# z and v on lanes of patch half and pixel in a convolution-and-GRU kernel: VectorE turns their product, GpSimd applies the norm's weight and bias

## The chip, the cores and the metric

The kernel runs as one program on one core of a Trainium2 chip. Five engines work side by side, each through its own queue in order: TensorE (PE, with its weight loads listed apart as PEld), VectorE (DVE), ScalarE (ACT), GpSimd (POOL) and SyncE (SP), which issues DMAs. The metric is the device time of one execution in microseconds (us). The time before is 5713.79 us, the median of three runs (5709.91 to 5723.35).

## The reference

The input x is (4, 64, 256, 256) in float32. Two residual layers follow each other.

```python
# layer 0
g = groupnorm(x)                                  # 32 groups, no weight
hidden = depthwise3x3(w1 @ g)                     # 64 -> 384 channels
q, k, v = split(hidden, 3)                        # 128 channels each
out = irfft2(rfft2(patches8x8(q)) * rfft2(patches8x8(k)))   # circular convolution in 8x8 patches
out = (out - mean_c(out)) / sqrt(var_c(out) + 1e-5) * ln_w + ln_b    # over the 128 channels of a pixel
x = x + w_out @ (v * out)
# layer 1
x = x + gru_over_columns(groupnorm(x))            # a scan over 256 columns, three neighbours each
```

The part in question is the norm over 128 channels, the gate `v * out`, and the projection by w_out with the residual. The normalised and gated values must get from one layout to another: the circular convolution leaves pixels on the partitions (lanes), and the projection contracts over channels, which therefore have to be on the lanes.

## The kernel before

Layer 0 runs in 32 blocks (`NBLK`) of 32 image rows, 128 patches of 8x8 pixels each. Layer 1 follows and is not touched. Every instruction is issued through a wrapper (`InOrder`, line 146) which keeps each engine's instructions in the order in which the program writes them, so the order of the Python statements is the order in each queue. All instructions carry line 158 in the profile; they are told apart by the names of their tiles.

A block n goes through these stages, in this order.

- Pointwise chunk 0, 1 and 2 (`pointwise`, line 353): 16 units each. A unit multiplies four patch columns by w1 into two PSUM banks, and ACT or VectorE copies them to h. The flag `vector` says which of the two copies.
- Circular stage 0, after chunk 0, and circular stage 1, after chunk 1 (`circular`, line 413). Each has four steps `sp`. A step transforms 16 channels of q and of k (two `transform`, 64 matmul records each) and VectorE multiplies them: three instructions `pr`, which the prediction calls a product set. ACT copies q from PSUM first; k stays in PSUM, except in the last step. Two steps together make an `inverse` (line 430), which goes back to pixels and is copied by ACT into z. It is issued one or more steps later (`pending`, `flush`).
- Values, after chunk 2 (`values`, line 450): eight steps k make v in the same layout as z. Beside them the next block's input xq is normalised (`normalize`, line 314: three quarters on ACT, one on VectorE; GpSimd sets the borders to zero).
- The norm over channels (`layer_norm`, line 469) is a generator. Each `next(norm)` in the main loop issues one more piece of it: VectorE's statistics of z during circular stage 1 and chunk 2; the mean and the variance, each through a matmul with the constant hh and back, during values; then 16 VectorE instructions on z (subtract the mean, multiply by the reciprocal root), from values into chunk 0 of the next block.
- Finish (`finish`, line 622), after chunk 0 of the next block: for each of four units u, PE transposes z and v, 128x128 at a time (`gate`, line 524). ACT applies ln_w and ln_b while it copies the transposed z, VectorE multiplies by the transposed v from PSUM, PE projects with w_out (`project`, line 566), VectorE adds to the residual xr loaded from x and takes statistics for layer 1, and SP stores to x1.

Before the change, z and v have pixels and half of the channels on the lanes: lane = channel half t x 64 pixels, columns = 128 patches x 64 channels. One lane therefore sees half of a pixel's channels, and hh joins the two halves.

PSUM is one ring of eight banks (`psum`, line 301). A pointwise unit or a transform takes two of them, an inverse four. PE can run ahead of the copies only as far as the ring is free. Work tiles come from a pool of seven. The matrices t of the transforms are loaded by SP four ahead of their use (`fetch`, line 340).

For images after the first, statistics of the next image are taken beside layer 0: GpSimd's queue loads pieces of x (`look`), and VectorE counts them (`count`).

Of the kernel before, what the change touches and what calls it, by code (L numbers as in the profile page):

```python
# [36 lines left out]
def channel_z(t, f):  # L37


    pair, rest = divmod(f, 16)  # L40
    c, s = divmod(rest, 4)
    return (2 * pair + t) * 16 + 4 * s + c
# [121 lines left out]
def tile_conv_then_gru(  # L164
# [10 lines left out]
    hh: bass.AP,  # L175
# [37 lines left out]
    with tc.tile_pool(name="xa", bufs=5) as xa, tc.tile_pool(name="sta", bufs=1) as sta, tc.tile_pool(  # L213
# [51 lines left out]
        ident = const.tile([P, P], F32, tag="ident", name="ident")  # L265
        make_identity(tc.nc, ident)
        hh_sb = const.tile([P, P], F32, tag="hh", name="hh_sb")
        nc.sync.dma_start(hh_sb, hh)
# [4 lines left out]
        wo_sb = const.tile([P, 2, C], F32, tag="wo", name="wo_sb")  # L273
        nc.sync.dma_start(wo_sb, w_out.rearrange("a f t c -> (a f) t c"))
        ln_sb = const.tile([P, 2, 2], F32, tag="ln", name="ln_sb")
        nc.sync.dma_start(ln_sb, ln.rearrange("a f n t -> (a f) n t"))
# [16 lines left out]
    with layer0 as s:  # L293
# [17 lines left out]
        z = big.tile([P, NP, NS], F32, tag="z", name="z")  # L311
        v = big.tile([P, NP, NS], F32, tag="v", name="v")
        lnst = big.tile([P, 2, NP // 2, 6], F32, tag="lnst", name="lnst")
# [63 lines left out]
        pending, later = [], []  # L377
# [35 lines left out]
        def circular(n, a, beside):  # L413
            ready = []
            for sp in range(4):
                ready.append(products(n, a, sp))
                beside(sp)
                if sp in (0, 2):
                    flush()
                if sp % 2:  # L420
                    at, pair = (n, 2 * a + sp // 2), ready[-2:]
                    pending.append(lambda at=at, pair=pair: inverse(*at, pair))
                    while later:
                        later.pop(0)()
# [5 lines left out]
        def inverse(n, pair, prods):  # L430

            pz = psum(4)
            for i in range(2):
                for part in range(2):
                    for t in range(2):
                        for c in range(4):
                            at = slice(32 * c, 32 * c + 32)
                            nc.tensor.matmul(
                                pz[t * 64 : t * 64 + 64, c, :],
                                lhsT=g_sb[at, part, i, :],  # L440
                                rhs=prods[t][i][at, part, :],
                                start=i == part == 0,
                                stop=i == part == 1,
                                tile_position=(32 * c, t * 64),
                            )
            nc.scalar.copy(
                z[:, :, 16 * pair : 16 * pair + 16], pz.rearrange("p x (f n) -> p n (x f)", n=NP)
            )

        def values(n, k, pv):  # L450

            m = matrix(n, 2, k)
            for f in range(8):
                for t in range(2):
                    nc.tensor.matmul(
                        pv[t * 64 : t * 64 + 64, f // 4, (f % 4) * P : (f % 4) * P + P],
                        lhsT=m[0:HALO, 2 * f + t, :],
                        rhs=h[:, 16 * k + 2 * f + t, :],
                        start=True,
                        stop=True,  # L460
                        tile_position=(0, t * 64),
                    )

        def keep_values(k, count, pv):
            nc.scalar.copy(
                v[:, :, 8 * k : 8 * (k + count)], pv.rearrange("p x (f n) -> p n (x f)", n=NP)
            )

        def layer_norm(n):

            st = lnst

            def statistics(a, p0, p1):

                for p in range(p0, p1):
                    nc.vector.bn_stats(
                        st[:, a, p, :],
                        z[:, 2 * p : 2 * p + 2, 32 * a : 32 * a + 32].rearrange("p n f -> p f n"),
                    )

            for i in range(4):
                statistics(0, 16 * i, 16 * i + 16)
                yield
            statistics(1, 0, 8)
            yield
            statistics(1, 8, 50)
            yield
            statistics(1, 50, NP // 2)
            m = work(f"lnm_{n}", (P, 8, NP))
            total, mean, d, var, rstd = m[:, 0], m[:, 1], m[:, 2:4], m[:, 4], m[:, 5]  # L490
            by = st.rearrange("p a i (e k) -> p a (i e) k", e=2)
            nc.vector.tensor_tensor(total, by[:, 0, :, 1], by[:, 1, :, 1], ALU.add)
            yield
            pm = psum()
            nc.tensor.matmul(pm[:, 0, 0:NP], lhsT=hh_sb, rhs=total, start=True, stop=True)
            nc.vector.tensor_copy(mean, pm[:, 0, 0:NP])
            nc.vector.tensor_tensor(
                d,
                by[:, :, :, 1],
                mean.rearrange("p (x n) -> p x n", x=1).to_broadcast([P, 2, NP]),  # L500
                ALU.subtract,
            )
            nc.vector.tensor_tensor(d, d, d, ALU.mult)
            nc.vector.scalar_tensor_tensor(d, by[:, :, :, 2], 1.0 / 32, d, ALU.mult, ALU.add)
            nc.vector.tensor_tensor(var, d[:, 0], d[:, 1], ALU.add)
            yield
            pv = psum()
            nc.tensor.matmul(pv[:, 0, 0:NP], lhsT=hh_sb, rhs=var, start=True, stop=True)
            nc.scalar.activation(rstd, pv[:, 0, 0:NP], AF.Sqrt, bias=eps, scale=1.0)
            nc.vector.reciprocal(rstd, rstd)  # L510
            yield
            for u in range(4):
                for g in range(2):
                    at = slice(g * NJ + 16 * u, g * NJ + 16 * u + 16)
                    for part, what in ((mean, ALU.subtract), (rstd, ALU.mult)):
                        nc.vector.tensor_tensor(
                            z[:, at, :],
                            z[:, at, :],
                            part[:, at].rearrange("p (n x) -> p n x", x=1).to_broadcast([P, 16, NS]),
                            what,  # L520
                        )
                    yield

        def gate(n, u):

            ys = []
            for g in range(2):
                p0 = g * NJ + 16 * u
                pz, pv = psum(), psum()
                for src, ps in ((z, pz), (v, pv)):  # L530
                    for i in range(8):
                        nc.tensor.transpose(
                            ps[:, i // 4, (i % 4) * P : (i % 4) * P + P],
                            src[:, p0 + 2 * i : p0 + 2 * i + 2, :].rearrange("p n f -> p (n f)"),
                            ident,
                        )
                y = work(f"y{g}_{n}_{u}", (P, 8, 2, 64))
                for t in range(2):
                    nc.scalar.activation(
                        y[:, :, t, :],  # L540
                        pz.rearrange("p x (i t k) -> p (x i) t k", t=2, k=64)[:, :, t, :],
                        AF.Identity,
                        bias=ln_sb[:, 1, t : t + 1],
                        scale=ln_sb[:, 0, t : t + 1],
                    )
                nc.vector.tensor_tensor(
                    y.rearrange("p i t k -> p (i t k)"),
                    pv.rearrange("p x k -> p (x k)"),
                    y.rearrange("p i t k -> p (i t k)"),
                    ALU.mult,  # L550
                )
                ys.append(y)
            return ys
# [3 lines left out]
        def residual(n, u):  # L557
            xr = work(f"xr_{n}_{u}", (P, 8, P))
            b, r0, c0 = n // 8, (n % 8) * 32 + (u // 2) * 8, (u % 2) * P
            for g in range(2):  # L560
                nc.sync.dma_start(
                    xr[g * C : (g + 1) * C], x[b, :, r0 + 16 * g : r0 + 16 * g + 8, c0 : c0 + P]
                )
            return xr

        def project(n, u, ys, xr):
            po = psum()
            for t in range(2):
                for p in range(2):
                    at = slice(p * 64, p * 64 + 64)  # L570
                    for g in range(2):
                        nc.tensor.matmul(
                            po[g * 64 : g * 64 + 64, p, :],
                            lhsT=wo_sb[at, t, :],
                            rhs=ys[g][at, :, t, :],
                            start=t == 0,
                            stop=t == 1,
                            tile_position=(p * 64, g * 64),
                        )
            grid = xr.rearrange("p r (i q c) -> p q i r c", q=2, c=8)  # L580
            for p in range(2):
                nc.vector.tensor_tensor(
                    grid[:, p],
                    po[:, p, :].rearrange("p (i r c) -> p i r c", r=8, c=8),
                    grid[:, p],
                    ALU.add,
                )
            if u == 0:
# [369 lines left out]
```

## Time and profile before

One execution was profiled.

| | us |
|---|---|
| median of three runs | 5713.79 |
| span of the profiled execution | 5733.1 |
| PE busy | 5456.4 |
| VectorE busy | 4085.7 |
| ACT busy | 3473.5 |
| GpSimd busy | 689.1 |
| layer 0's blocks, from about 130 to 4290 us: VectorE busy | 2955.9 |

The span is the time from the first to the last instruction; the page gives no other time of the profiled execution, and it stands 0.34% above the median. "Busy" counts the time in which an engine has at least one instruction under way. Matmuls are pipelined, so a busy PE is not PE at its peak. The names are read as output<-inputs: `z<-z,lnm` is a VectorE instruction that reads z and the norm's mean or factor and writes z; `psring<-h,t` is a transform or a set of values; `psring<-pr,g_sb` an inverse; `psring<-ident,z` a transpose; `psring<-y,wo_sb` a projection. A matmul in float32 leaves two records, a transpose one. In timeline rows the first two numbers are start and length in us, then engine, operation, names, shapes, count, and in brackets the idle time before and what ended it.

### The profile page before, as it was taken

The page shows a single profiled execution, that of the slowest core. Times are in us where ns is not written, and L with a number is a line of the kernel's source. Part 1 is how long each engine was busy: PE and PEld are TensorE (multiplying, and loading weights), DVE is VectorE, ACT ScalarE, POOL GpSimd, SP SyncE. Part 2 cuts the span into 40 slices and gives each one's busy share as a digit, 9 for nine tenths or more (in the row PEclk, how much of TensorE's full clock was granted, in tenths as well). Part 3 has the DMA queues.
Part 4 walks back from the last instruction along what each step waited for, and adds up shares of the span by engine and source line. Part 5 has one row for each costly group of instructions (what it writes and reads, how often), then busy time and mean ns, then how long its engine had stood idle before and what let it go on. Part 6 is the DMA issues. An engine that isn't in the chain of part 4 may idle for free.

```text
span 5733.1 us, 278945 instructions
## 1 busy us (share of the span) xinstructions
PE 5456.4 (95%) x127204; PEld 4746.7 (83%) x127204; DVE 4085.7 (71%) x9593; ACT 3473.5 (61%) x4604; POOL 689.1 (12%) x1261
## 2 busy tenths in 40 slices
PE   4999999999999999999999999999989999999999
PEld 3888888888788788888878888888869999999998
DVE  4777777777767777777776676667667777777777
ACT  3656666665566566666556656666546666666665
POOL 0000000000000000000000000000003333333333
PEclk9999999999999999999999999999999999999999
DMA  7555555555555555555555444555443333333332
GB/s 254 149 150 152 153 159 151 145 139 159 154 152 148 151 150 158 153 153 139 156 157 151 131 140 135 149 137 131 130 112 112 100 98 96 102 100 98 102 99 70
DMA packets 536798, 784.74 MB, mean 137 GB/s; under 512 B 33388, under 2 KB 427536, under 8 KB 533232
## 3 DMA queue, kind: packets, MB, share of 16 engines
q1 hardware_dynamic: 501776, 600.89, 38.6%
q0 software_dynamic: 33552, 165.43, 9.1%
q8 instruction: 996, 16.32, 1.2%
q14 instruction: 186, 1.52, 0.1%
q10 hardware_dynamic: 288, 0.58, 0.0%
HBM read 622.72 MB, written 144.05 MB: 134 GB/s over the span
## 4 chain that ended last, share of the span: by engine, by line
PE 85%; issue 4%; ACT 4%; DMA 3%; DVE 2%; POOL 0%; SPq 0%; POOLq 0%; ACTq 0%; DVEq 0%
PE psring L158 62%; PE pshz L158 8%; PE pshr L158 8%; PE psni L158 6%; DMA t<-t_all 3%; PE pshn L158 2%; ACT v L158 2%; ACT z L158 1%; ACT h L158 1%; DVE lnst L158 0%; DVE pr L158 0%; DVE z L158 0%; ACT xq L158 0%; POOL raw L158 0%; DVE n L158 0%
## 5 line engine op out<-in xcount | busy, mean ns | idle before, releaser
L158 PEld LDWEIGHTS psring<-h,t 100*32 100x32 f32 x40960 | 1334.3, 115 | 287.8 <-issue 198.4
L158 PE MATMUL psring<-h,t 100*32 100x128 f32 x40960 | 1444.2, 274 | 101.0 <-issue 36.9
L158 PEld LDWEIGHTS psring<-w_sb,xq 64*100 64x100 f32 x24576 | 1356.8, 163 | 86.8 <-issue 57.8
L158 PE MATMUL psring<-w_sb,xq 64*100 64x128 f32 x24576 | 1402.0, 271 | 25.9 <-issue 12.0
L158 ACT COPY h<-psring 100x1024 f32<-100x1024 f32 x1274 | 1206.2, 1026 | 167.9 <-PE psring L158 161.6
L158 DVE TENSOR_TENSOR pr<-psring,q 128x512 f32<-128x512 f32 (+1 forms) x576 | 462.3, 858 | 333.5 <-PE psring L158 270.5
L158 DVE BATCH_NORM_STATS2 lnst<-z 128x6 f32<-128x64 f32 x4096 | 546.0, 217 | 117.7 <-ACT z L158 117.7
L158 DVE TENSOR_TENSOR z<-z,lnm 128x1024 f32<-128x1024 f32 x512 | 612.7, 1218 | 8.8
L158 ACT COPY q<-psring 128x1024 f32<-128x1024 f32 x256 | 259.3, 1013 | 527.3 <-PE psring L158 434.3
L158 PE MATMUL pshr<-st,wi 64*64 64x144 f32 (+7 forms) x12240 | 527.7, 271 | 22.4 <-DVE st L158 13.8
L158 ACT COPY z<-psring 128x2048 f32<-128x2048 f32 x128 | 238.9, 1867 | 505.4 <-PE psring L158 505.4
L158 PE MATMUL pshz<-st,wi 64*64 64x144 f32 (+7 forms) x12240 | 527.4, 270 | 6.0 <-issue 4.7
L158 PE MATMUL psni<-st,wi 64*64 64x144 f32 (+7 forms) x12240 | 527.0, 271 | 4.4 <-issue 3.1
L158 ACT ACTIVATE z<-pshz,b_rz 128x288 f32<-128x288 f32 (+7 forms) x510 | 242.5, 476 | 462.0 <-PE pshz L158 462.0
L158 ACT ACTIVATE y<-psring,ln_sb 128x512 f32<-128x512 f32 x512 | 372.1, 780 | 201.9 <-PE psring L158 199.9
L158 PE MATMUL psring<-pr,g_sb 32*64 32x512 f32 x8192 | 486.6, 600 | 5.4 <-issue 5.4
L158 PEld LDWEIGHTS psni<-st,wi 64*64 64x64 f32 x12240 | 456.8, 133 | 30.1 <-issue 12.1
L158 PEld LDWEIGHTS pshr<-st,wi 64*64 64x64 f32 x12240 | 438.4, 133 | 37.2 <-issue 18.2
L158 PEld LDWEIGHTS pshz<-st,wi 64*64 64x64 f32 x12240 | 445.0, 133 | 15.7 <-issue 14.2
L158 DVE COPY h<-psring 100x1024 f32<-100x1024 f32 x262 | 320.1, 1222 | 171.7 <-PE psring L158 167.7
L158 DVE TENSOR_TENSOR y<-psring,y 128x1024 f32<-128x1024 f32 x256 | 312.4, 1221 | 135.3 <-ACT y L158 134.3
L158 DVE SCALAR_TENSOR_TENSOR g<-z,xn 128x288 f32<-128x288 f32 (+7 forms) x510 | 227.2, 446 | 236.3 <-ACT z L158 232.5
(101 smaller groups left out, 7536.5 us busy)
## 6 DMA issues: line engine op xcount, KB each, us to landing
t<-t_all SPq DMA_DIRECT2D x768, 400.0 KB
xq<-in_xh POOLq DMA_DIRECT2D x128, 800.0 KB, 4.6
xr<-in_x SPq DMA_DIRECT2D x256, 256.0 KB
x<-xr SPq DMA_DIRECT2D x256, 256.0 KB
raw<-x SPq DMA_DIRECT2D x128, 256.0 KB
raw<-x SPq DMA_DIRECT2D x256, 128.0 KB
out<-raw SPq DMA_DIRECT2D x128, 256.0 KB
out<-raw SPq DMA_DIRECT2D x256, 128.0 KB
```

The costliest lines, as they stand in the source:

```text
L158: return self.tc.keep_in_program_order(got(*args, **kwargs))
```

## The change

z and v now have the patch half (64 patches each) and the pixel on the lanes, and all 128 channels of 64 patches in the columns. A lane sees all the channels of its pixel. For that, the inverse and the values write 64 patches to each half of the lanes, with twice as many matmuls of half as many columns. The statistics need no matmul with hh. After VectorE has subtracted the mean and multiplied by the factor, GpSimd multiplies by ln_w and adds ln_b, both broadcast along the patches. VectorE multiplies by v in this layout and then turns the product in 32x32 blocks, in place, which puts 32 channels of a pixel group on 32 lanes. The projection contracts over 32 lanes at a time, four row groups and four channel blocks, so that two projections of 64 matmul records replace four of 16, and the 128x128 transposes on PE go.

The order changes with it. The norm's generator has 30 pieces: s0 to s7 scale one eighth of z each (two VectorE instructions, two of GpSimd), y0 to y7 multiply by v, two behind, and eight turn the product. Pieces s0 to s4 with y0 and y1 lie beside values, the other s and y beside chunk 0 of the next block (y7 after it), the turns beside circular stage 0 and the start of chunk 1. The projections move from between chunk 0 and circular stage 0 into chunk 1 (after units 0 and 7), with the loads of xr and the stores to x1. VectorE gets 12 of the 48 copies to h instead of 8.

```diff
 def inverse(n, pair, prods):
     pz = psum(4)
-    for i in range(2):
-        for part in range(2):
-            for t in range(2):
-                for c in range(4):
...
+    for t in range(2):
+        for i in range(2):
+            for part in range(2):
+                for g in range(2):
+                    for c in range(4):
+                        at = slice(32 * c, 32 * c + 32)
+                        nc.tensor.matmul(
+                            pz[g * 64 : g * 64 + 64, c, t * 256 : t * 256 + 256].rearrange(
+                                "p (s n) -> p s n", n=NJ
+                            ),
+                            lhsT=g_sb[at, part, i, :],
+                            rhs=prods[t][i][at, part].rearrange("p (s g n) -> p g s n", g=2, n=NJ)[:, g],
...
 def values(n, k, pv):
     m = matrix(n, 2, k)
-    for f in range(8):
-        for t in range(2):
+    for f in range(16):
+        for g in range(2):
             nc.tensor.matmul(
+                pv[g * 64 : g * 64 + 64, f // 8, (f % 8) * NJ : (f % 8) * NJ + NJ],
+                lhsT=m[0:HALO, f, :],
+                rhs=h[:, 16 * k + f, g * NJ : g * NJ + NJ],
...
 def layer_norm(n):
...
-    pm = psum()
-    nc.tensor.matmul(pm[:, 0, 0:NP], lhsT=hh_sb, rhs=total, start=True, stop=True)
...
+    def scaled(i):
+        at, f = where(i)
+        for part, what in ((mean, ALU.subtract), (rstd, ALU.mult)):
+            nc.vector.tensor_tensor(
+                z[:, at, f], z[:, at, f],
+                part[:, at].rearrange("p (n x) -> p n x", x=1).to_broadcast([P, 32, 32]), what)
+        for j, what in ((0, ALU.mult), (1, ALU.add)):
+            nc.gpsimd.tensor_tensor(
+                z[:, at, f], z[:, at, f],
+                ln_sb[:, j, f].rearrange("p (x f) -> p x f", x=1).to_broadcast([P, 32, 32]), what)
+
+    def gated(i):
+        at, f = where(i)
+        nc.vector.tensor_tensor(v[:, at, f], v[:, at, f], z[:, at, f], ALU.mult)
+
+    for step in "s0 s1 s2 y0 s3 y1 s4 y2 s5 y3 s6 y4 s7 y5 y6 y7".split():
+        (scaled if step[0] == "s" else gated)(int(step[1]))
+        yield
+    for i in range(8):
+        chunk = v[:, 8 * i : 8 * i + 8].rearrange("p n f -> p (n f)")
+        nc.vector.transpose(chunk, chunk)
+        yield

-def gate(n, u):
...
 def project(n, u):
+    po = psum(4)
+    y = v.rearrange("p n (b k) -> p b n k", k=32)
+    for b in range(4):
+        for r in range(4):
+            for s in range(2):
+                n0 = 32 * u + 16 * s
+                nc.tensor.matmul(
+                    po[s * 64 : s * 64 + 64, r].rearrange("p (n k) -> p n k", k=32),
+                    lhsT=wo_sb[32 * r : 32 * r + 32, b, :],
+                    rhs=y[32 * r : 32 * r + 32, b, n0 : n0 + 16],
...
 for n in range(NBLK + 1):
...
     for unit in range(16):
-        pointwise(n, 0, unit, unit in (5, 9) if norm else unit % 2)
+        pointwise(n, 0, unit, unit in (3, 8, 13) if norm else unit % 2)
+        if unit % 2:
+            go()
...
     def beside_first(sp):
+        go((2, 1, 1, 1)[sp])
...
+    go()
     circular(n, 0, beside_first)
+    if n:
+        parts[0] = residual(n - 1, 0)
...
     for unit in range(16):
-        pointwise(n, 1, unit, unit in (5, 8, 11, 14))
+        pointwise(n, 1, unit, unit in (2, 5, 8, 11, 14))
+        if unit == 0 and n:
+            po = project(n - 1, 0)
+            add_residual(0, po, parts[0])
+        if unit in (1, 3, 4, 5):
+            go()
+        if unit == 3:
+            flush()
+            if n:
+                leave(n - 1, 0, parts[0])
+                parts[1] = residual(n - 1, 1)
+        if unit == 7 and n:
+            po = project(n - 1, 1)
+            add_residual(1, po, parts[1])
+        if unit == 9 and n:
+            leave(n - 1, 1, parts[1])
...
     for unit in range(16):
-        pointwise(n, 2, unit, unit in (6, 14))
+        pointwise(n, 2, unit, unit in (1, 4, 6, 15))
...
     for k in range(8):
...
+        if k >= 1:
+            go()
```

Here `go()` issues the next piece of the norm, `add_residual` is VectorE's addition of a projection to xr, and `leave` its statistics and the stores.

## The prediction

> **What bounds the kernel now.** I read the page's busy shares, its chain, and then one block (32 alike; VectorE's reciprocals follow each other every 130.2 us on average) by windows and timeline.
>
> ```profile
> PE 5456.4 (95%) x127204; PEld 4746.7 (83%) x127204; DVE 4085.7 (71%) x9593; ACT 3473.5 (61%) x4604; POOL 689.1 (12%) x1261
> PE 85%; issue 4%; ACT 4%; DMA 3%; DVE 2%; POOL 0%; SPq 0%; POOLq 0%; ACTq 0%; DVEq 0%
> ```
>
> TensorE is busy 95% and holds 85% of the chain. In two stretches of the block at 1951 us (columns: stretch, length, then busy us of PE, weight loads, DVE, ACT, POOL, clock, DMA):
>
> ```profile
> 2036.80:2057.80 21.00, 20.74 (x371) 19.97 (x367) 20.76 (x19) 18.68 (x18) 1.35 (x6) 1.00 0.72 164
> 2057.80:2077.90 20.10, 20.10 (x182) 15.51 (x184) 16.27 (x18) 12.87 (x18) 0.00 (x0) 1.00 0.39 81
> ```
>
> The second is transposing, gating and projecting: PE full. But in the first, where z is normalised, VectorE is full too (20.76 of 21): there the two engines are even, and what is added to VectorE shows. Work by work:
>
> ```profile
> 2057.79 1.09 PE L158 MATMUL psring<-ident,z 128*128 128x128 f32 x8
> ...
> 2064.93 1.95 PE L158 MATMUL psring<-y,wo_sb 64*64 64x512 f32 x16
> 2066.80 1.09 PE L158 MATMUL psring<-ident,z 128*128 128x128 f32 x8
> ...
> 2000.27 3.69 PE L158 MATMUL psring<-pr,g_sb 32*64 32x512 f32 x64
> ...
> 2028.90 0.49 PE L158 MATMUL psring<-lnm,hh_sb 128*128 128x128 f32 x2
> 2029.32 3.71 PE L158 MATMUL psring<-h,t 100*64 100x128 f32 x64
> ...
> 2033.67 0.20 PEld L158 LDWEIGHTS psring<-h,t 100*64 100x64 f32 x4
> ...
> 2036.89 4.82 DVE L158 TENSOR_TENSOR z<-z,lnm 128x1024 f32<-128x1024 f32 x4
> ```
>
> GpSimd does no arithmetic in layer 0. How it gets on beside VectorE is seen in layer 1:
>
> ```profile
> 4905.54 0.39 POOL L158 COPY xt<-xn 64x256 f32<-64x256 f32 x1
> 4905.57 0.66 DVE L158 SCALAR_TENSOR_TENSOR g<-z,xn 128x268 f32<-128x268 f32 x1 [0.38 <-ACT z L158]
> ...
> 5086.36 0.44 DVE L158 SCALAR_TENSOR_TENSOR g<-z,xn 128x266 f32<-128x266 f32 x1 [0.51 <-ACT z L158]
> 5086.36 0.68 POOL L158 COPY xt<-xn 64x256 f32<-64x256 f32 x1
> 5086.76 0.58 DVE L158 TENSOR_TENSOR n<-n,z 128x266 f32<-128x266 f32 x1
> ```
>
> g takes 0.44 alone, 0.66 behind a copy begun 0.03 us earlier: it ends 0.30 us after the copy, which is the time of its 268 elements. At 5086 g is first, and the copy of 0.39 takes 0.68, ending 0.25 after g; n, queued next, takes 0.58 and ends 0.30 after the copy. So a VectorE instruction with two inputs in SBUF and a GpSimd instruction that reads SBUF run one after the other; only their start (0.14 us) overlaps. All 24 VectorE instructions that normalise and gate here are of that kind, and all 16 of GpSimd's.
>
> **The change part by part, per block.**
>
> *PE, removed.* 128 transposes: 64 from 2057.79 to 2064.93 and 32 in each 3.65 us after, 14.4 us. Two hh matmuls, each 0.42 to the next start: 0.8.
>
> *PE, added.* The inverse has 64 matmuls of 256 columns for 32 of 512, the same columns on eight tiles: 64 records pace at 57.6 ns now, 128 would need 28.8; the four-tile transforms come to 30 (384 records in 11.5 us): 0, at worst +0.6. The projection takes two runs of 64 records like the inverse's (7.3 us) for four of 1.87 (7.5): 0. Values: 64 columns instead of 128 and twice the records. The row of four weight loads in 0.20 us (about 0.13 each) shows the two tiles' loads side by side, a pair per 55 ns, against the 57.6 ns that a pair then needs: 0, at worst twice the stage, +14.8. I take +0.4, by that row. PE: -14.8.
>
> *ACT* loses 16 activations of 0.78 us and four h copies of 1.03. It is off the chain (4%): 0.
>
> *VectorE* trades eight multiplies y<-psring,y (1.22) for eight from SBUF (1.22), keeps 16 on z, gains four h copies (4.9) and eight block transposes. No row shows a transpose: 0.71 us by the 1600-element xq scaling (1.11), 2.05 by the 64-element statistics (128 ns apart), I take 1.22 as the tensor_tensor of the same 1024. Statistics fall from 128 by 128 ns to 64 by about 195: -3.9. Projection add and bn_stats stay eight each. The norm's small steps shrink by about 1. Busy in all: 92 us a block now (2955.9 from 130 to 4290 us, over 32), about 102 after, before any waiting.
>
> *GpSimd* gets 16 tensor_tensor of 1024. Layer 1's of 512 take 1.09 to 1.29, so 2.03 (start counted once) to 2.57. I take 2.04, as the new operands are aligned alike; 1.90 of it excludes VectorE (1.09 less 0.14, doubled).
>
> *The new wait.* Product i of v and z waits for GpSimd's two passes over block i. Behind it in VectorE's queue stand the h copies of units 3, 8 and 13, then the first product of the circular stage; PE waits for the copies' banks, for h, and for the products. Behind GpSimd's passes stand the border memsets of the next block (needed at units 4, 8 and 12) and a load of seen, which has the circular stage to land in.
>
> Count from VectorE's first instruction on z (T; 2036.89 here). If the two exclude each other: 24 of 1.09 plus 16 of 1.90 make 56.6, with the first start and the hand-overs 58, the copies and xq lying beside GpSimd. Taken in turns, the copies of units 3, 8 and 13 end near T+32, T+45 and T+52 and the last gate at T+58; the memsets are through by T+20, before they count. Then come the three instructions of the first product set (2.42), two transposes (2.4) and the second set (2.4): T+65.2, when the first inverse can start. PE now ends the pointwise at T+20.9; T comes 1.0 earlier (the variance no longer passes PE, and ACT's root is free after its first scaling of xq), so 21.9, and with six transforms (1.85 each, 11.1) PE would be there at T+33. Lateness 32.2 us. Later, in the second pointwise run, the copies behind adds and statistics hold banks: 0 to 4, I take 2.
>
> *Moved:* the projection with its eight x loads and eight x1 stores on SP goes behind the first circular stage; same count and size. Matrices are fetched four ahead of it, so 0; without that cover, waits like the 14.5 us in all that PE has on t now.
>
> Sum per block: -14.8 + 32.2 + 2 = +19.4; 31 blocks: +601. The last block has nothing beside it: from T to layer 1's norm 45.6 us now (4244.4 to 4290.0); after, 57 + 9.8 (transposes) + 14.6 (two projections at half clock) + 5.7 (adds, statistics) = 87: +41. In all +642 on the span of 5733.1: 6375; the span stands 0.34% above the median of the runs, so 6355.
>
> **The clock, weighed.** After a wait PE is slow:
>
> ```profile
> 4264.81 1.97 PE L158 MATMUL psring<-ident,v 128*128 128x128 f32 x8 [6.07 <-DVE y L158]
> ```
>
> Eight transposes take 1.97 instead of 1.04 us, the next eight 1.92. My sum pays this only in the tail: in the blocks the first four transforms end by T+61.3 even so, before the second product set needs them (T+62.8). The Trainium skill (TensorE: Matmul & The Clock Gate, "HAM oscillation") warns of gaps over about 3 us; charging 1.7 us for each of a block's three new waits would add some 158 us, an estimate by that page.
>
> **The place of the passes, weighed.** On VectorE the same 16 passes would be 16 x 1.20 = 19.3 us, and the last gate would end at T+53 instead of T+58: the rows say that GpSimd's help costs more than it saves here. The Trainium skill (GPSIMD Engine Reference, "Engine selection") sends elementwise work on a tile to VectorE and speaks against this part of the change; its 4497 ns for 2048 elements would make an estimated 2.25 us of a pass instead of 2.04, some 3 us a block more.
>
> **Rivals.**
>
> 1. *GpSimd does not hold VectorE up* (a gain). Then GpSimd's passes alone set the pace: 2.4 + 8 x 4.2 + 1.2 = 37.2, lateness 11.4, 1 for banks; -2.4 a block, -75, tail +20: about 5660. For it: the busy time that GpSimd adds, 33 us a block, is a quarter of the block. Against: the three rows above. It decides when the last gate ends by T+39.
>
> 2. *PE alone counts*, the rest hidden: -14.8 x 31 = -459, 5255. Against: VectorE's work alone from T (24 at 1.20, three copies, xq: 33.7 us) outlasts PE's 21.9, which leaves 8 us of lateness if nothing else is slow.
>
> 3. *Dearer passes*: GpSimd at 2.57 (+6.3) and a transpose at 2.05 (+1.7, and 2 for banks): +10 a block, +325 with the tail: 6680.
>
> **How the numbers follow.** Forecast 0.70; rival 1 and what lies near it 0.13, of which 0.03 falls within 0.2% (about what a measurement of this kernel can tell from no change); rival 2 0.02; rival 3 0.15. Faster 0.12, same 0.03, slower 0.85. The range goes up to rival 3, and down to a partial exclusion (the last gate at T+45: 13 us less a block, 400 in all): 5950 to 6690.
>
> **What would show it.** In the changed profile: block period near 150 us; VectorE's z and v instructions at 2 to 3 us instead of 1.22, GpSimd's at 2 to 3; PE idle on DVE h and DVE pr after each block's values, over 20 us together; its clock below 1 there; a set of values still about 1.85 us. It is wrong if z<-z stays at 1.22 beside GpSimd, or if values double.

## The result and the profile after

The changed kernel takes 7016.98 us (median of four runs, 7015.38 to 7022.98) where the kernel before takes 5711.85 in the same series (5709.27 to 5723.35). The ratio is 1.2285, with a 95% interval of 1.2268 to 1.2303. The forecast was slower, 6355 us, with a range of 5950 to 6690. The sign was right; the loss is 1305 us where 642 were forecast.

The page of the changed kernel: span, busy shares, TensorE's granted clock by slices in tenths, the chain.

```profile
span 7016.5 us, 305020 instructions
PE 5448.0 (78%) x141412; PEld 4868.1 (69%) x141412; DVE 5238.6 (75%) x7928; ACT 3002.9 (43%) x3965; POOL 2406.1 (34%) x1771
PEclk9888888888888888888888888888888799999999
PE 46%; DVE 30%; ACT 7%; issue 6%; POOL 6%; DMA 3%; SPq 0%; DVEq 0%; ACTq 0%; POOLq 0%
```

PE's share of the chain falls from 85% to 46%, and VectorE's rises from 2% to 30%. PE is busy for as long as before (5448.0 against 5456.4 us; in a block of layer 0, 126.4 against 126.0), although the change takes some 459 us of work from it, by the prediction's 14.8 a block: what was saved came back as longer records at a lower clock. The row PEclk stands at 8 in nearly all of layer 0, where it stood at 9 before.

The costliest groups (line, engine, operation, names, shapes, count, then busy us, mean ns of one, idle time before and what ended it):

```profile
L157 PE MATMUL psring<-w_sb,xq 64*100 64x128 f32 x24576 | 1612.2, 288 | 897.3 <-DVE h L157 851.3
L157 POOL TENSOR_TENSOR z<-z,ln_sb 128x1024 f32<-128x1024 f32 x512 | 1722.2, 3370 | 406.7 <-DVE z L157 386.7
L157 DVE TENSOR_TENSOR z<-z,moments 128x1024 f32<-128x1024 f32 x512 | 1320.4, 2589 | 8.8
L157 PE MATMUL psring<-pr,g_sb 32*64 32x256 f32 x16384 | 693.1, 453 | 248.0 <-DVE h L157 205.6
L157 DVE COPY h<-psring 100x1024 f32<-100x1024 f32 x389 | 469.6, 1209 | 332.6 <-PE psring L157 328.5
L157 DVE TENSOR_TENSOR v<-v,z 128x1024 f32<-128x1024 f32 x256 | 479.4, 1882 | 72.7 <-POOL z L157 72.7
L157 DVE STREAM_TRANSPOSE v<-v 128x1024 f32<-128x1024 f32 x256 | 310.7, 1225 | 0.0
L157 DVE TENSOR_SCALAR xq<-xq,sc 128x1600 f32<-128x1600 f32 x32 | 97.9, 3060 | 0.0
```

VectorE's z instructions last 2.59 us and the gates 1.88, where the prediction's row had 1.22; GpSimd's 3.37. The h copies, which read PSUM and have one input, stay at 1.21. But the scaling of xq, one input in SBUF, goes from 1.11 to 3.06.

One step of the alternation, from the timeline (start, length, engine, names, count):

```profile
2644.32 6.46 POOL L157 TENSOR_TENSOR z<-z,ln_sb 128x1024 f32<-128x1024 f32 x2 [1.69 <-DVE z L157]
2645.22 6.64 DVE L157 TENSOR_TENSOR z<-z,moments 128x1024 f32<-128x1024 f32 x2
2651.78 1.21 DVE L157 TENSOR_TENSOR v<-v,z 128x1024 f32<-128x1024 f32 x1
2651.94 6.55 POOL L157 TENSOR_TENSOR z<-z,ln_sb 128x1024 f32<-128x1024 f32 x2 [1.17 <-DVE z L157]
2652.92 1.21 DVE L157 COPY h<-psring 100x1024 f32<-100x1024 f32 x1
```

Two instructions of each engine take 6.64 us together, 3.32 a pair. VectorE's own share of it is 1.09 (the prediction's figure) to 1.2 (two in a row without GpSimd), so one GpSimd pass holds it up for 2.1 to 2.2 us. The gate that follows begins 0.16 us before GpSimd's next pass and takes its 1.21; so does the h copy at 2652.92, which lies wholly beside that pass. Over the whole of the norm in this block (columns: stretch, length, busy us of PE, weight loads, DVE, ACT, POOL, clock, DMA):

```profile
2619.83:2684.10 64.27, 35.82 (x809) 34.77 (x807) 61.73 (x30) 22.68 (x21) 55.00 (x22) 0.79 0.16 53
```

VectorE and GpSimd both look nearly full, but much of that is waiting for the other. By the lengths above, VectorE's own work here (24 passes, three copies, xq) is some 32 us of its 61.7, and GpSimd's (16 passes of 2.2) some 36 of its 55.0; both are estimates. The last gate ends 64.2 us after the first z instruction. The busy column counts such waiting as work.

By stages of PE (mean length in us over 29 blocks, worked out from the starts of PE's groups in the timeline; the forecast stages are the prediction's terms put where they fall; the second and third pointwise run are chunks 1 and 2):

| stage | before | forecast | after | miss |
|---|---|---|---|---|
| chunk 0 and circular 0 | 56.7 | 67.0 | 70.6 | +3.6 |
| chunk 1 | 17.8 | 27.1 | 38.3 | +11.2 |
| circular 1 | 19.4 | 19.4 | 21.1 | +1.7 |
| chunk 2 | 19.9 | 19.9 | 23.8 | +3.9 |
| values | 16.4 | 16.0 | 16.9 | +0.9 |
| block | 130.2 | 149.4 | 170.7 | +21.3 |

The largest miss is in the second pointwise run. PE and VectorE there:

```profile
2706.72 1.71 PE L157 MATMUL psring<-w_sb,xq 64*100 64x128 f32 x16 [0.20 <-DVE xr L157]
2708.36 0.65 PE L157 MATMUL psring<-pr,g_sb 32*64 32x256 f32 x4
2713.59 5.80 PE L157 MATMUL psring<-pr,g_sb 32*64 32x256 f32 x124 [4.58 <-DVE h L157]
```

```profile
2705.98 1.29 DVE L157 TENSOR_TENSOR xr<-psring,xr 128x512 f32<-128x512 f32 x2 [1.48 <-DMA xr<-in_x]
2709.99 1.29 DVE L157 TENSOR_TENSOR xr<-psring,xr 128x512 f32<-128x512 f32 x2 [2.73 <-DMA xr<-in_x]
2711.20 1.23 DVE L157 STREAM_TRANSPOSE v<-v 128x1024 f32<-128x1024 f32 x1
2712.36 1.18 DVE L157 COPY h<-psring 100x1024 f32<-100x1024 f32 x1
```

The inverse needs the banks of unit 2, whose copy to h (2712.36) stands in VectorE's queue behind the residual's additions; these wait for the load of xr. PE waits 4.58 us. The inverse's remaining 124 records then take 5.80 us. The granted clock in that stretch is 0.63:

```profile
2713.59:2719.39 5.80, 5.79 (x126) 3.75 (x126) 5.19 (x7) 0.00 (x0) 0.54 (x1) 0.63 0.58 156
```

### The profile page after: what moved, and what is told of

The parts are those of the page before. It is cut to its first block, busy times and chain, and to the rows that moved or that the text cites. A ratio compares the mean times of both kernels' runs of the same rounds, so it can differ in the third digit from the quotient of the medians.

```text
span 7016.5 us, 305020 instructions
## 1 busy us (share of the span) xinstructions
PE 5448.0 (78%) x141412; PEld 4868.1 (69%) x141412; DVE 5238.6 (75%) x7928; ACT 3002.9 (43%) x3965; POOL 2406.1 (34%) x1771
## 4 chain that ended last, share of the span: by engine, by line
PE 46%; DVE 30%; ACT 7%; issue 6%; POOL 6%; DMA 3%; SPq 0%; DVEq 0%; ACTq 0%; POOLq 0%
PE psring L157 26%; DVE z L157 15%; PE pshr L157 6%; PE pshz L157 6%; POOL z L157 6%; PE psni L157 5%; DVE v L157 4%; DVE pr L157 4%; ACT h L157 3%; DMA xr<-in_x 3%; DVE h L157 3%; ACT z L157 2%; PE pshn L157 2%; DVE xr L157 1%; DVE xq L157 1%
## 5 line engine op out<-in xcount | busy, mean ns | idle before, releaser
L157 PE MATMUL psring<-w_sb,xq 64*100 64x128 f32 x24576 | 1612.2, 288 | 897.3 <-DVE h L157 851.3
L157 PEld LDWEIGHTS psring<-w_sb,xq 64*100 64x100 f32 x24576 | 1505.5, 176 | 1045.4 <-DVE h L157 878.1
L157 POOL TENSOR_TENSOR z<-z,ln_sb 128x1024 f32<-128x1024 f32 x512 | 1722.2, 3370 | 406.7 <-DVE z L157 386.7
L157 PEld LDWEIGHTS psring<-h,t 100*32 100x32 f32 x49152 | 1434.3, 122 | 326.0 <-ACT h L157 149.6
L157 DVE TENSOR_TENSOR z<-z,moments 128x1024 f32<-128x1024 f32 x512 | 1320.4, 2589 | 8.8
L157 PE MATMUL psring<-pr,g_sb 32*64 32x256 f32 x16384 | 693.1, 453 | 248.0 <-DVE h L157 205.6
L157 PEld LDWEIGHTS psring<-pr,g_sb 32*64 32x64 f32 x16384 | 464.5, 160 | 442.8 <-DVE h L157 235.0
L157 DVE COPY h<-psring 100x1024 f32<-100x1024 f32 x389 | 469.6, 1209 | 332.6 <-PE psring L157 328.5
L157 DVE TENSOR_TENSOR v<-v,z 128x1024 f32<-128x1024 f32 x256 | 479.4, 1882 | 72.7 <-POOL z L157 72.7
L157 POOL TENSOR_TENSOR raw<-raw,st 128x512 f32<-128x512 f32 x256 | 303.6, 1186 | 529.0 <-DVE st L157 408.4
```

Source lines behind the costliest of these rows:

```text
L157: return self.tc.keep_in_program_order(got(*args, **kwargs))
```

## The experiments

My theory after the result: (a) exclusion of VectorE and GpSimd, dearer than forecast; (b) two waits for copies that stand behind other work in VectorE's queue; (c) the slow clock after every wait, paid in the blocks. Rivals: the gates wait only for GpSimd's results; VectorE is simply full; the new order and shapes are slow in themselves. Where a kernel ran once, the kernel before ran once beside it; those single runs lie between 5667 and 5752 us, so a single run tells 2% and no less.

**1. The passes on VectorE.**

```diff
-                    nc.gpsimd.tensor_tensor(
+                    nc.vector.tensor_tensor(
                         z[:, at, f],
```

> The sixteen weight and bias instructions of a block go from GpSimd to VectorE; nothing else changes. Theory (VectorE and GpSimd exclude each other, so that GpSimd's passes cost VectorE more than they would on VectorE itself): z on VectorE back at 1.20 us, the last gate ends at T+53 (40 instructions of 1.20, three copies, xq) in place of T+64 in the profile of the changed kernel; 11 us less a block, 340 in all, and somewhat more where TensorE's clock stays up: 6600 to 6680 us. Rival (GpSimd doesn't hold VectorE up, VectorE is just full): 19 us more on VectorE in each block, 600 in all: 7600 us.

Measured: 6683.3 us. This is at the upper edge of what was expected. z is back at 1.22, the 512 passes moved take 1.23 each, and xq is back at 1.11.

```profile
L157 DVE TENSOR_TENSOR z<-z,ln_sb 128x1024 f32<-128x1024 f32 x512 | 627.2, 1225 | 17.6
L157 DVE TENSOR_TENSOR z<-z,moments 128x1024 f32<-128x1024 f32 x512 | 623.6, 1218 | 8.7
L157 DVE TENSOR_SCALAR xq<-xq,sc 128x1600 f32<-128x1600 f32 x32 | 35.4, 1107 | 0.0
```

The last gate of a block ends 52.8 us after the first z instruction (53 expected) and the block period falls from 170.6 to 160.6 us. An engine that does all the work alone is faster than the two together: the rival that VectorE is merely full falls.

**2. No passes at all, and 3. the passes on another tile.** In 2 the loop that issues them is left out; 3 keeps GpSimd's work but puts it on a small tile (`aside`, a view of the statistics' tile `seen`), so that no other engine needs its results. Neither applies weight and bias.

```diff
+            aside = seen.rearrange("p (n f) -> p n f", f=32)
...
-                    nc.gpsimd.tensor_tensor(
-                        z[:, at, f],
-                        z[:, at, f],
-                        ln_sb[:, j, f].rearrange("p (x f) -> p x f", x=1).to_broadcast([P, 32, 32]),
-                        what,
-                    )
+                    for _ in range(2):
+                        nc.gpsimd.tensor_tensor(
+                            aside,
+                            aside,
+                            ln_sb[:, j, f].rearrange("p (x f) -> p x f", x=1).to_broadcast([P, 16, 32]),
+                            what,
+                        )
```

> The weight and bias of the norm are not applied at all; GpSimd does no arithmetic in layer 0. Theory: z and v at 1.2 us, the last gate ends at T+34, 30 us earlier, and the block is shorter by at least that: 31 times 30 is 930, 6090 us or less. It gives what is left of the change when GpSimd's passes cost nothing: by the predicted sum (PE 14.8 us less a block, 8 us of lateness, 2 for banks) 5570; what it stays above 5570 belongs to the other steps (waits in the second pointwise run, the clock). Rival (the new order and the projection cost, not the passes): above 6600 us.

> GpSimd does the same number of elements of multiplication and addition, in twice as many instructions of 512, on the small tile of the statistics: VectorE never waits for their results (the weight and bias are so not applied to z). Theory (the two engines exclude each other in time): z on VectorE stays above 2 us while GpSimd works, GpSimd's queue lasts some 35 us of holding, and the time stays near the changed kernel's: 6700 to 7000 us. Rival (the gates only wait for GpSimd's result, there is no exclusion): z and v at 1.2 us, and the time of the kernel without the passes, some 900 us less than the changed kernel's.

Measured: 6040.0 us without the passes, 6697.3 with the passes aside. The block periods are 140.6 and 161.0 us. The rows of the second:

```profile
L157 POOL TENSOR_TENSOR seen<-seen,ln_sb 128x512 f32<-128x512 f32 x1024 | 2013.1, 1966 | 171.0 <-ACT moments L157 93.0
L157 DVE TENSOR_TENSOR z<-z,moments 128x1024 f32<-128x1024 f32 x512 | 1060.9, 2082 | 8.8
L157 DVE TENSOR_TENSOR v<-v,z 128x1024 f32<-128x1024 f32 x256 | 446.6, 1764 | 0.0
L157 DVE TENSOR_SCALAR xq<-xq,sc 128x1600 f32<-128x1600 f32 x32 | 64.7, 2022 | 0.0
```

Nothing waits for GpSimd's results here, and still z takes 2.08 us and the kernel loses 657 us to the one without passes: that loss is exclusion, shown without any dependence. Of the 20.5 us a block, 19.0 arise before the last gate (it ends 51.7 us after the first z instruction, 32.7 without the passes), and in that stretch VectorE is never idle, so it is not a wait for a DMA from GpSimd's queue either. The rival that the gates only wait for results falls. A pass of 512 holds VectorE up for about 1.1 us (z instructions follow each other every 2.2), half of what 1024 cost. The passes on z itself cost 977 us in all, so about two thirds is exclusion as measured in 3; the rest comes with the dependence of the gates and the order of turns. Part of it can be seen: in 3 GpSimd is still at its passes when the last gate has ended, while on z all sixteen have to come before it (64.2 us against 51.7). 3 does not divide it further, since its passes have another size and place.

**4. The copy of unit 2 in the second pointwise run on ScalarE.**

```diff
-                pointwise(n, 1, unit, unit in (2, 5, 8, 11, 14))
+                pointwise(n, 1, unit, unit in (5, 8, 11, 14))
```

> In the second pointwise run the h copy of unit 2 goes from VectorE to ScalarE; the four others stay. Theory (the last inverse of the first circular stage waits for that copy, which stands behind the residual's additions in VectorE's queue, and these wait for the late load of xr): the 5.5 us of PE idle on DVE h there and its slow clock go, 5 to 8 us a block, 160 to 250 in all: 6770 to 6860 us. Rival (the wait passes on to the next copy on VectorE, that of unit 5): within 0.5% of 7017 us.

Measured: 6840.2 us, 177 less. The second pointwise run falls from 38.3 to 33.1 us, PE's idle on DVE h in it from 5.5 to 0.6, and the inverse behind it is no longer slow:

```profile
2636.26 3.71 PE L157 MATMUL psring<-pr,g_sb 32*64 32x256 f32 x128
```

All 128 records take 3.71 us here, 124 of them 5.80 after the wait: the shape is not slow, the clock was. The two terms are worth 4.9 us (wait) and about 2 (clock) a block, more than the 5.2 by which the run gets shorter; the wait did not pass on to unit 5, but PE now waits 0.8 us on v, the last turns ahead of the second projection, and is slow after it in some blocks.

**5. No passes, and both copies on ScalarE**: as 2 and 4, with unit 1 of the third run too (`unit in (4, 6, 15)`).

> As the kernel without GpSimd's passes (weight and bias are not applied), and the h copies of unit 2 in the second pointwise run and of unit 1 in the third go from VectorE to ScalarE, so that neither inverse there waits for a copy that stands behind other work of VectorE. Theory (what that kernel, 6040 us, stays above the predicted 5570 is two waits of PE for these copies and the slow clock that PE has in the inverses after them): the inverse in the second run falls from 5.8 to 3.7 us and that in the third from 5.4 to 3.7, PE idle on DVE h falls by 5.5 and 2.0 us, about 5 + 3.5 us a block, 260 in all: 5750 to 5800 us. Rival (the waits pass to the next copy, or the inverse is slow by its 256-column shape and not by the clock): above 5950 us.

Measured: 5867.7 us, 172 less than without the passes, where 240 to 290 were expected (7.3 us a block, 8.5 expected). The third pointwise run comes to 20.0 us (23.5 in experiment 2, 19.9 in the kernel before the change): that term was right and is gone. The second run is at 33.3 and not at 27: its second projection waits for turns that VectorE has still to do (0.7 us a block), and runs slowly after it, where 64 records take 3.69 us in the changed kernel:

```profile
2300.63 4.77 PE L157 MATMUL psring<-v,wo_sb 32*64 32x512 f32 x62 [1.69 <-DVE v L157]
```

In eight other blocks these 62 records take 5.9 to 6.5 us. So the change without its passes and without those two waits is still slower than the kernel before: 2.2% above the 5742.8 us of the run beside it, little more than a single run tells. What its blocks show is waiting (3.8 us a block on h copies of VectorE in the first run, and the second run); that the order of work makes up the whole difference is not shown here.

**6 to 9. A version in which the parts are placed by these findings.** First, one instruction with two scalars per patch for mean and factor, 16 of the 64 patches on ScalarE, weight and bias on VectorE, z begun earlier:

```diff
+                        nc.scalar.activation(z[:, n], z[:, n], AF.Identity, bias=d[:, one], scale=rstd[:, one])
...
+                        nc.vector.tensor_scalar(
+                            z[:, n], z[:, n], mean[:, one], rstd[:, one], ALU.subtract, ALU.mult
+                        )
```

> A version with weight and bias applied and nothing on GpSimd: the mean and the factor are applied per patch by one instruction with two scalars (48 patches on VectorE, 16 on ScalarE) in place of two passes of 1024; weight, bias and gate are VectorE passes over 8 patches; this work begins in the third pointwise run, 8 us before TensorE comes to the values, instead of after the first of them; the turns go beside the first circular stage; the copies of unit 2 and unit 1 go to ScalarE as in the other kernel. Theory (VectorE's time up to the first inverse is what decides): VectorE needs about 38 us from 8 us before T, so the last gate ends near T+30 and the first inverse waits about 2 us; block period 121 to 126 us, 5450 to 5600 us. If a small instruction of 128 elements takes 0.2 us and not 0.15: 3 us a block more, 5700. Rival (PE's wait for banks comes back because ScalarE has most copies): above 5800 us.

Measured: 6185.6 us, a miss; it lies where the rival had it. Eight instructions of 128 elements take 2.13 us on VectorE, 0.27 each, and 3.18 on ScalarE, 0.40 each: all 64 patches on VectorE would need 17 us a block, against 18 for the passes that they replace. On ScalarE they also delay the copies of v, for which PE waits (some 3 us a block in the values), and PE waits 2.6 us for ScalarE's h copies in the third run. I had taken 0.15 without a row. How the miss of some 20 us a block divides was not worked out.

Then the weight goes into the taps of v, once, and the bias divided by the weight is the only pass left (a weight of zero is replaced by 1e-20, so that the product stays the bias times v):

```diff
+        nc.vector.tensor_scalar(rest, ln_sb[:, 0], 0.0, 1e-20, ALU.is_equal, ALU.mult)
+        nc.vector.tensor_tensor(ln_sb[:, 0], ln_sb[:, 0], rest, ALU.add)
+        nc.vector.reciprocal(rest, ln_sb[:, 0])
+        nc.vector.tensor_tensor(ln_sb[:, 1], ln_sb[:, 1], rest, ALU.mult)
...
+            nc.vector.tensor_tensor(wd[at, 2 * E : 3 * E], wd[at, 2 * E : 3 * E], ln_sb[at, 0], ALU.mult)
```

> Nothing on GpSimd, and weight and bias applied for any values: the weight is multiplied into the taps of v once, at the start, on VectorE, and the bias, divided by the weight, is one more VectorE pass on z (three on z and the gate: 32 instructions of 1.15 us to the next start, 36.8 us a block). The norm's small steps follow the statistics in the third pointwise run, so z is begun 3 us before TensorE comes to the values, 7 us earlier than in the changed kernel. Two h copies on VectorE in the first pointwise run, two in each of the others; the turns beside the first circular stage; the projections after units 5 and 10 of the second pointwise run. Theory (VectorE's time to the first inverse and the queue order decide): last gate 41 us after the first z instruction, TensorE ready for the first inverse at 48, no lateness; block period 119 to 125 us, 5400 to 5570 us. Rival (waits for ScalarE's copies and the slow clock behind them, as in the version before): above 5711 us.

Measured: 6083.4 us; the rival held. VectorE did what was expected (the last gate ends 42 us after the first z instruction, 41 expected), but ScalarE's queue did not:

```profile
2182.30 0.35 ACT L157 ACTIVATE moments<-seen,eps 128x64 f32<-128x64 f32 x1 [2.90 <-DVE seen L157]
2182.55 3.73 ACT L157 COPY h<-psring 100x1024 f32<-100x1024 f32 x4
2186.34 0.91 PE L157 MATMUL psring<-h,t 100*64 100x64 f32 x12 [4.66 <-ACT h L157]
```

I had placed the norm's root after unit 11. It waits 2.90 us for VectorE's statistics, four copies to h stand behind it, and PE waits 4.66 us for the last of them. The third version moves it behind unit 15, and takes h copies from VectorE where its queue is long:

```diff
-                pointwise(n, 0, unit, unit in (5, 11) if norm else unit % 2)
+                pointwise(n, 0, unit, False if norm else unit % 2)
...
-                pointwise(n, 1, unit, unit in (9, 14))
+                pointwise(n, 1, unit, unit == 9)
...
-                if unit in (7, 8, 11):
+                if unit in (7, 8, 15):
                     go()
```

> As the version with the weight in the taps, and three moves in the queues: no h copy on VectorE in the first pointwise run (two before), only that of unit 9 in the second (units 9 and 14), and the norm's small steps with the root on ScalarE after unit 15 of the third run, not after unit 11, so that the copies of units 12 to 15 no longer stand behind a root that waits for VectorE. Theory (PE's idle of 4.3 us on DVE h in the first run, of 3.9 us ahead of the second circular stage and of 4.3 us on ACT h ahead of the values, and the slow clock after each, come from these places in the queues): about 17 us a block less, 5500 to 5650 us, below the kernel before. Rival (ScalarE can't make all the copies at PE's pace, or VectorE's later start on z moves the wait to the first inverse): above 5850 us.

Measured: 5663.4 us, 420 less, with the kernel before at 5667.3 beside it. That kernel took 5751.9 beside the second version, so the block tells it better: 128.5 us against 140.8, some 380 in 31 blocks. Three moves in the order, with the same work. The fourth puts work behind the product sets that nobody needs before them:

```diff
+STEPS = "s0 s1 s2 y0+y1 s3 y2+s4 y3 s5 y4 s6 s7 y6 t0 t1 t2 t3 y5 y7 t4 t5 t6 t7"
...
-                go(2)
+                go((1, 2, 2, 2)[sp])
...
-                pointwise(n, 1, unit, unit == 9)
+                pointwise(n, 1, unit, unit in (9, 14))
+                if unit < 4:
+                    go()
```

> As the version of 5663 us (weight in the taps, nothing on GpSimd), and the last three gates, y6 ahead of the first turns and y5 and y7 behind the third product set, go behind the first product set, the last four turns into the second pointwise run; one h copy (unit 1) on VectorE in the first pointwise run; in the second the copy of unit 14 on VectorE ahead of the residual's statistics, and the next image's third piece counted at unit 7, so that its fourth has landed before the second circular stage. Theory (what is left above PE's own time stands in VectorE's queue ahead of the first product sets of both circular stages): first inverse 3 to 4 us earlier, the second circular stage 2, the end of the second run 1: 6 to 7 us a block, 5440 to 5520 us, 4% below the kernel before. Rival (the turns, now later, hold up the projections, or ScalarE is the bound): within 1% of 5663 us.

Measured: 5646.59 us (median of four runs, 5621.73 to 5668.83) against 5713.11 (seven, 5698.86 to 5731.62); ratio 0.988, interval 0.983 to 0.993. It is 1.2% below the kernel before, a small difference but clear of the interval, and a fifth below the changed kernel. I expected 4%. The rival held (within 1% of 5663), and 5663 to 5647 alone tells nothing: the block falls from 128.5 to 127.5 us where 6 to 7 were expected. Its page:

```profile
span 5641.5 us, 304638 instructions
PE 5120.1 (91%) x141412; PEld 4577.7 (81%) x141412; DVE 4370.4 (77%) x7970; ACT 3184.2 (56%) x4187; POOL 694.5 (12%) x1259
PEclk9999999999999999999999999999979999999999
```

The PE work that the change takes away shows when PE waits less: 5142.8 us busy in the third version and 5120.1 here, against 5448.0 with the same 141412 matmuls, and 5456.4 in the kernel before. That is 336 of the 459 us. Chunk 0 is at 16.3 us, of which 1.8 are waits, and chunk 2 at 19.9, as in the kernel before; chunk 1 stays at 31.5, 4.4 us above the 27.1 of the forecast. One of these is a wait for a copy on VectorE, 1.2 are waits for copies on ScalarE, and 1.2 are waits that the profile puts down to nothing. What these last are is open.

## Why the prediction missed

The table's 21.3 us a block are 660 us in 31 blocks; together with 5 us more in the tail they are the whole miss. Four terms of the sum failed, the largest of them the 2 us for banks.

**The sign and the mechanism** were right: exclusion between VectorE and GpSimd, read from layer 1's 256-element copies, carries over to 1024-element passes (experiments 1 to 3). The values cost next to nothing, as said (16.9 us against 16.4, with 0.8 us of waits on issue), the h copies did lie beside GpSimd, the transposes take 1.225 us (1.22 taken), the statistics 196 ns (195), the tail grew from 45.6 to 91.2 us (by 46, 41 forecast).

**"1.90 of it excludes VectorE"** failed by size: 2.1 to 2.2 us, 3 to 5 us over sixteen passes. I had put together two layer-1 lengths from other shapes and taken the low end. The Trainium skill (GPSIMD Engine Reference, "Elementwise — side-by-side cycle accounting") states 4497 ns for 2048 elements; the prediction's estimate of 2.25 from it is close to what this trace shows.

**"The copies and xq lying beside GpSimd"** was right for the copies and wrong for xq: 3.06 us in place of 1.11, 2 us more. Its row had a sign of this: 1600 elements in 1.11 us is 0.69 ns each, where a pass of 1024 in 1.22 us takes 1.19 ns each, so it is not an instruction like the one-input copies (1024 in 1.21). The Trainium skill (SBUF — State Buffer, "SBUF: two separate sides") lists VectorE instructions in a two-port performance mode beside those with two SBUF inputs as holders of the shared port; the xq rows of the changed kernel (3.06) and of experiment 1 (1.11) agree. Both terms together make the last gate T+64.2, not T+58, and the first inverse starts at T+68.3 and is held until T+70.6, not T+65.2. The stage misses by only 3.6 us in the table, less than this and the slow inverse behind it add up to. A part of the difference is that T came earlier: PE began chunk 0 at T+8.6 on average, T+6.5 before the change, so 2.1 us where the prediction had 1.0. The rest was not traced, and that the stage came out so close is in part luck.

**"0 to 4, I take 2" for the banks in the second pointwise run**, with **"so 0" for what was moved**, failed most: 11.2 us a block more than forecast. I counted the moved projection's instructions and DMAs, but not that the copy of unit 2 would stand behind its additions, that these wait for xr, and that the inverse needs that copy's banks. VectorE waits 151.7 us for xr in all. Experiment 4 took 177 us away by moving one copy, 5.2 of the 11.2 us. In what is left PE still waits 1.7 us for h copies of ScalarE, 0.8 for the residual's additions, 0.8 for turns and 0.6 for h copies of VectorE; the remaining 2 us stay open. The same in the third run (unit 1 behind statistics, 3.9 us) I had not named; experiment 5 removed it.

**"My sum pays this only in the tail"** failed: PE's busy time did not fall. After each of a block's three waits an inverse is slow, and so are the transforms of circular 1 (third row), here in the block shown above:

```profile
2690.44 5.73 PE L157 MATMUL psring<-pr,g_sb 32*64 32x256 f32 x124 [1.67 <-DVE pr L157]
2713.59 5.80 PE L157 MATMUL psring<-pr,g_sb 32*64 32x256 f32 x124 [4.58 <-DVE h L157]
2737.62 12.36 PE L157 MATMUL psring<-h,t 100*32 100x128 f32 x384 [1.83 <-ACT h L157]
2765.63 5.39 PE L157 MATMUL psring<-pr,g_sb 32*64 32x256 f32 x124 [2.04 <-DVE h L157]
```

Full clock is 3.7 us. Over the 31 blocks the three inverses take 4.9, 5.6 and 4.9 us on average, some 4.4 us a block too much. The transforms of circular 1 pay it too: 384 records take 12.36 us here, 11.5 by the prediction's row, and this stage misses by 1.7. The Trainium skill (TensorE: Matmul & The Clock Gate, "HAM oscillation"), which the prediction weighed, gave an estimate of 1.7 us for each of three waits; measured are 1.7 to 2.1 in this block and 1.2 to 1.9 on average. The page warns of gaps over about 3.4 us; here shorter ones counted as well: of the waits in layer 0 that began at full clock, all 91 of over 3 us were followed by a half clock, 44 of 56 between 1.75 and 2.25 us, and 20 of 190 between 0.75 and 1.75. Leaving it out was the wrong choice, made because the first transforms after the gates looked covered; the inverses behind the waits are not.

**Rivals.** Rival 1 fell with GpSimd's rows, rival 2 with it: without any passes and without two of the waits the kernel takes 5868, so even uncontended it isn't PE alone. Rival 3 had dearer passes (2.57) and dearer transposes (2.05): the first came half true, the second not; its 6680 was too low since it, like the forecast, had next to nothing for the waits in the second and third pointwise runs and nothing for the clock in the blocks. The range was built from the prices of instructions alone and took in no queue order that I had not read.

## What to carry to other kernels

Do not split a chain of float32 tensor_tensor passes in SBUF between VectorE and GpSimd to balance their busy shares: here they took turns, and with the same passes on VectorE alone the kernel was 5% faster. When a stage is moved, list for each queue what comes to stand behind it and whose banks that holds, since three moves in the order were worth 12.3 us a block with the same matmuls and the same passes; and charge the slow clock after waits of TensorE, as here after all of over 3 us and most of about 2.

## What the runs showed of the hardware

- A GpSimd tensor_tensor holds VectorE for 2.1 to 2.2 us per 1024 elements and about 1.1 per 512, on whatever tile; it holds a one-input tensor_scalar from SBUF too (1.11 to 3.06 us), and not a copy from PSUM (1.21).
- VectorE's 32x32 turn of 128x1024 float32 in place takes 1.225 us, as long as a tensor_tensor of that size.
- An instruction of 128 elements with two per-lane scalars takes 0.27 us on VectorE, an activation of 128 elements 0.40 us on ScalarE, in a row of eight: 64 of the first take 17 us, two whole passes over the same elements 18.
- The same matmul records take 5.80 us (124 of them) after a wait of 4.6 us, at a granted clock of 0.63, and 3.71 (all 128) without one.
